# A hand-ordered opening, weight units loaded a head ahead, and where the parting of the turned weights stands

## The chip, the cores and the metric

The kernel runs on one core of one Trainium2 chip. The metric is device time in microseconds (us) of one execution. TensorE (PE) multiplies, VectorE (DVE) and ScalarE (ACT) work element by element, GpSimd (POOL) does so too[...], and SyncE (SP) issues nearly all DMA transfers. Each engine works through its own queue of instructions in order; semaphores make one wait for another.

## What is computed

One transformer layer with adaptive layer norm, all in f32, for 4 batches of 512 tokens and 256 channels. From a 4 x 256 conditioning vector `c` come six modulation vectors; two shift, two scale, two gate:

```python
mod = (_silu(L0_c) @ L0_wmod).reshape(4, 6, 1, -1)
sa, ca, ga, sb, cb, gb = (mod[:, i] for i in range(6))
ga = (2 * (ga >= 0) - 1) * jnp.maximum(jnp.abs(ga), 0.25)   # gb likewise
h = _layernorm(x) * (1 + ca) + sa
x = x + ga * attention(h)        # 16 heads of 128, causal
h = _layernorm(x) * (1 + cb) + sb
x = x + gb * ffn(h)              # top 2 of 8 experts, a shared one, a dense core
```

Attention projects h to q, k and v per head, takes a causal softmax of the scores and mixes v with it, and an output matrix W_O sums over the heads. The mixture of experts follows; the change doesn't touch its arithmetic.

## The kernel before

f32 accuracy is kept by splitting: a tensor is cast to a shorter format (`hi`), what the cast lost is subtracted out (`lo`, the helper `rest`, line 148), and three products replace one (`mm3`, lines 138 to 142: lo*hi, hi*lo, hi*hi). Weights arrive as units of 128 x 512 in one of two `stage` buffers and are split into one of ten `wu` buffers by `load_unit` (line 185): the cast by POOL (by ACT for the first three), the rest by POOL. A unit `wqk` holds a head's q and k weights; `wv` and `wo` hold two heads each.

The opening loads x of batch 0 in two pieces, `cT`, and the modulation weights (`wm`, six pieces of 256 KB). `sc` is the SiLU of `cT`: an exponential on ACT, three small steps on DVE. `modulation(0)` (line 301) multiplies it by the first pieces into `pt_mod`, whence `modT`, the shift and scale columns. `normed` (line 348) takes statistics on DVE (`bn_stats`, `bn_aggr`), 1/sqrt on POOL (`rstd`), and normalises on DVE (`xn`); `modulated` (line 378) transposes xn on TensorE into PSUM (`ptn`), applies modT there, and splits the result into `hTh` and `hTl`.

Then 64 heads follow in groups of four heads, batch after batch (line 981: heads 0 to 3 of batch 0, of batch 1, and so on). In the loop over n (line 1028) TensorE's order is written by hand:

- `weights` (line 471): four blocks of scores, 128 to 512 columns wide, in two PSUM banks taken in turn. For each: the row minimum of the negated scores on DVE (`nmax`, line 488, which frees the bank), the exponential with its row sum on ACT, its inverse on DVE, and the scaling on POOL (line 503). The generator yields after each block, so that other work stands between them.
- between the blocks: whatever `later[n]` holds, then q and then k of the next head (`project`, line 448).
- after the fourth block: `values` for the current or the next pair of heads; `finish` (line 1001, the output products of the head mixed one head before); and `mixed` (line 540), the products of v with the weights of the head three before.
- `turned` (line 506): the weights are transposed in blocks of 32 on DVE (`T`), stored to DRAM by four transfers (`moved`) and loaded again as `aT`, fully transposed. `part_one(-2)` splits the aT of two heads before (`parted`, line 531: a cast of 128 x 1152 by ACT to `aTh`, a rest by POOL).

Work beside the heads: the next batch's normalisation in heads 0 to 3 of the first group; the gates in head 1 (`make_gates`, line 319, on 4 partitions x 512); the gates' rows read back from DRAM (`gate_rows`) in heads 2 to 5; `modulation(1)` in head 6; five units loaded in heads 0 to 2; from head 18 on, feed-forward weights are split and put back to DRAM (`PART_AT`, line 102).

Only PE's order is fixed (line 151); on DVE and ACT it is fixed for the opening alone, and elsewhere a scheduler places each instruction on its engine by its own estimate of times, within `issue_after`, which keeps an instruction behind a given one.

Of the kernel before, what the change touches and what calls it, by code (L numbers as in the profile page):

```python
# [11 lines left out]
F32 = mybir.dt.float32  # L12
# [11 lines left out]
HG = 4  # L24
# [73 lines left out]
EARLY = 2  # L98


TO_PART = tuple(u for u, (_, in_parts) in UNITS.items() if in_parts)
PART_AT = (18, 20, 22, 24, 26, 28, 34, 36, 38, 40, 42)
# [11 lines left out]
def adaln_attention_moe_kernel(  # L114
# [51 lines left out]

    load_x(0, 2)
    cT = const.tile([P, DC, B], F32, tag="cT", name="cT")
    nc.sync.dma_start(cT, c_t.rearrange("(c p) b -> p c b", p=P))
# [15 lines left out]
    def load_unit(src, nm: str, early: bool = False):  # L185

        st = work.tile([P, 512], F32, tag="stage", name=f"st_{nm}")
        nc.sync.dma_start(st, src)
        u = const.tile([P, 2, 512], F32R, tag="wu", name=nm, bufs=10)
        hi, lo = u[:, 0], u[:, 1]  # L190
        if early:
            nc.scalar.copy(hi, st)
        else:
            nc.gpsimd.tensor_scalar(hi, st, 1.0, 1.0, ALU.mult, ALU.mult)
        rest(nc.gpsimd, lo, st, hi)
        return hi, lo
# [62 lines left out]
    sc_e = small.tile([P, DC, B], F32, bufs=1, tag="silu_e", name="sc_e")  # L259
    exp_c = nc.scalar.activation(sc_e, cT, AF.Exp, scale=-1.0)  # L260
    nc.vector.tensor_scalar(sc_e, sc_e, 1.0, None, ALU.add)
    nc.vector.reciprocal(sc_e, sc_e)
    sc = small.tile([P, DC, B], F32, bufs=1, tag="silu", name="sc")
    nc.vector.tensor_mul(sc, cT, sc_e)

    ct = const.tile([P, C_END], F32, tag="cols", name="cols")
    nc.gpsimd.dma_start(ct, cols)
    b1 = ct[:, C_B1:C_B2]
    with tc.issue_after(exp_c.ins):
        nc.scalar.activation(gb1, b1[:, :NCH], AF.Gelu)  # L270
    load_wm(0)
    wqk_u[0] = load_unit(wqk[0], "wqk0", True)
    wv_u[0] = load_unit(wv[0], "wv0", True)
    load_wm(1)
    load_wm(2)
    wqk_u[1] = load_unit(wqk[1], "wqk1", True)
    for b in range(1, B):
        load_x(b)
# [3 lines left out]
    nc.vector.memset(router_w, 0.0)  # L282
    nc.sync.dma_start(router_w[:, :, :E], router.rearrange("p (c n) -> p c n", n=E))
# [8 lines left out]
    nc.vector.memset(mask[:, : NT - 1, :], 0.0)  # L292
    make_causal_mask(nc, mask[:, NT - 1, :], mask_val=MASKED)
    maskf = mask.rearrange("p t k -> p (t k)")
    def mod_w(c: int, f: int, n: int) -> bass.AP:
# [5 lines left out]
    def modulation(which: int):  # L301
        pt = psum.tile([P, 4, B], F32, tag="pj", name=f"pt_mod_{which}", bufs=3)
        for i in range(4):
            for c in range(DC):
                nc.tensor.matmul(
                    pt[:, i, :],
                    lhsT=mod_w(c, 3 * D * which + i * P, P),
# [3 lines left out]
                )  # L311
        m = modT[:, 4 * which : 4 * which + 4, :]
        nc.vector.tensor_copy(m[:, :2, :], pt[:, :2, :])
        nc.vector.tensor_scalar(m[:, 2:, :], pt[:, 2:, :], 1.0, None, ALU.add)


    gates_d = dram.tile([B, 2, D], F32, tag="gates", name="gates_d")

    def make_gates():
        pm = psum.tile([B, 2, D], F32, tag="pj", name="pm", bufs=3)  # L320
        for i in range(2):
            for c in range(DC):
                nc.tensor.matmul(
                    pm[:, i, :],
                    lhsT=sc[:, c, :],
                    rhs=mod_w(c, (3 * i + 2) * D, D),
                    start=(c == 0),
                    stop=(c == DC - 1),
                )
        g = work.tile([B, 2, D], F32, tag="kh", name="g_raw")  # L330
        nc.scalar.copy(g, pm)
        sgn = work.tile([B, 2, D], F32, tag="kl", name="g_sgn")
        nc.vector.tensor_scalar(sgn, g, 0.0, 2.0, ALU.is_ge, ALU.mult)
# [866 lines left out]
```

## Time and profile before

| | |
|---|---|
| median of 3 runs | 810.0 us (808.84 to 810.09) |
| the profiled execution | 809.29 us, of which 807.5 us is the span of its instructions |
| TensorE busy | 775.5 us, 96% |
| DVE, ACT, POOL busy | 594.7, 490.9, 521.7 us |
| granted TensorE clock, mean | 0.986 |
| row minimum of the scores on DVE (line 488) | 256 x 478 ns |
| scaling of the weights on POOL (line 503) | 256 x 543 ns |
| cast of aT on ACT, its rest on POOL | 64 x 1159 ns, 64 x 2687 ns |
| moved to DRAM, and back as aT | 2.8 and 3.9 us from issue to landing |

The profile is of one execution. A row gives start and duration, the engine (PEld is TensorE's loading of the stationary operand), the source line, `out<-in` by the program's names, shapes, and in brackets how long the engine had been idle and what ended it. Matmuls are pipelined: two rows overlap, and the distance of their starts is what one costs. An f32 product that isn't split into three appears as two records.

### The profile page before, as it was taken

How to read it: one execution, taken by the hardware profiler on the slowest of the kernel's cores; microseconds unless marked ns; L12 is line 12 of the kernel's file. 1: busy time of each engine (PE TensorE's matmuls, PEld its weight loads, DVE VectorE, ACT ScalarE, POOL GpSimd, SP SyncE). 2: the span in 40 equal slices, each digit the busy share in tenths (PEclk: the TensorE clock that was granted, in tenths of full speed). 3: DMA queues.
4: the chain of work that ended last, by engine and by line, in shares of the span. 5: the costliest groups of instructions: out<-in, count | busy, mean ns of one | idle time of the engine just before them, and what ended most of it. 6: DMA issues, size and time to landing. Idle time of an engine off the chain costs nothing. (4 is left out here: it accounts for less than half of the span.)

```text
span 807.5 us, 14122 instructions
## 1 busy us (share of the span) xinstructions
PE 775.5 (96%) x4487; PEld 671.9 (83%) x4487; DVE 594.7 (74%) x1734; ACT 490.9 (61%) x1184; POOL 521.7 (65%) x523
## 2 busy tenths in 40 slices
PE   6889999999999999999999999999997999989997
PEld 5669998999999999999999999998896866767775
DVE  5968788777777667676777677778898486785665
ACT  3556667666666655666666656666656333656663
POOL 4745566896767579786758886566546155655675
PEclk9999999999999999999999999999998899999999
DMA  7465354665666667675556765545575332312221
GB/s 236 112 190 152 111 156 128 184 180 160 199 192 182 182 204 220 174 213 177 177 175 186 191 178 151 162 137 160 147 227 156 106 124 86 105 53 77 55 86 58
DMA packets 73218, 124.12 MB, mean 154 GB/s; under 512 B 8996, under 2 KB 51252, under 8 KB 73144
## 3 DMA queue, kind: packets, MB, share of 16 engines
q1 hardware_dynamic: 73112, 123.21, 52.3%
q8 instruction: 36, 0.59, 0.3%
q14 instruction: 38, 0.31, 0.1%
q0 software_dynamic: 32, 0.02, 0.0%
HBM read 73.05 MB, written 50.14 MB: 153 GB/s over the span
## 5 line engine op out<-in xcount | busy, mean ns | idle before, releaser
L148 POOL TENSOR_TENSOR aT<-aT,aTh 128x1152 fp32r<-128x1152 f32 x64 | 172.0, 2687 | 115.5 <-ACT aTh L535 115.4
L503 POOL TENSOR_SCALAR e<-e,inv 128x128 f32<-128x128 f32 (+3 forms) x256 | 135.7, 543 | 69.3 <-DVE inv L502 67.2
L498 ACT ACTIVATE e<-e,nmax 128x128 f32<-128x128 f32 (+3 forms) x256 | 143.9, 564 | 45.4 <-DVE nmax L488 44.5
L535 ACT CAST aTh<-aT 128x1152 fp32r<-128x1152 f32 x64 | 74.2, 1159 | 134.8 <-DMA aT<-moved 81.3
L488 DVE CUSTOM_DVE_ANT_0 e<-ps,mask 128x128 f32<-128x128 f32 (+3 forms) x256 | 120.1, 478 | 23.8 <-PE ps L482 14.6
L518 DVE STREAM_TRANSPOSE T<-e 128x384 f32<-128x384 f32 (+2 forms) x256 | 100.3, 445 | 7.8 <-POOL e L503 7.8
L148 DVE TENSOR_TENSOR zl<-pz,zh 128x512 fp32r<-128x512 f32 x64 | 44.0, 688 | 52.8 <-ACT zh L553 52.7
L140 PE MATMUL ps<-kh,ql 128*128 128x256 f32 (+2 forms) x192 | 71.2, 371 | 6.3 <-DVE nmax L488 6.2
L140 PE MATMUL po<-wo,zl 128*128 128x256 f32 x256 | 73.1, 285 | 0.6 <-DVE zl L148 0.6
L141 PE MATMUL po<-wo,zh 128*128 128x256 f32 x256 | 72.0, 281 | 0.0
L142 PE MATMUL po<-wo,zh 128*128 128x256 f32 x256 | 72.0, 281 | 0.0
L140 PE MATMUL pv<-wv,hTl 128*128 128x256 f32 x256 | 71.8, 281 | 0.0
L141 PE MATMUL pv<-wv,hTh 128*128 128x256 f32 x256 | 71.6, 280 | 0.0
L142 PE MATMUL pv<-wv,hTh 128*128 128x256 f32 x256 | 71.5, 279 | 0.0
L863 POOL TENSOR_TENSOR oacc<-oacc,part 128x512 f32<-128x512 f32 x28 | 40.9, 1462 | 43.5 <-DVE part L859 36.8
L502 DVE RECIPROCAL inv<-tot 128x1 f32<-128x1 f32 x256 | 40.2, 158 | 37.2 <-ACT e L498 29.6
L141 PE MATMUL ps<-kl,qh 128*128 128x256 f32 (+2 forms) x192 | 65.5, 341 | 0.2
L140 PE MATMUL pz<-aTh,vl 128*128 128x512 f32 (+2 forms) x192 | 65.5, 341 | 0.0
L141 PE MATMUL pz<-aT,vh 128*128 128x512 f32 (+2 forms) x192 | 65.4, 341 | 0.0
L142 PE MATMUL pz<-aTh,vh 128*128 128x512 f32 (+2 forms) x192 | 65.4, 340 | 0.0
L142 PE MATMUL ps<-kh,qh 128*128 128x256 f32 (+2 forms) x192 | 65.0, 339 | 0.0
L592 POOL TENSOR_TENSOR x<-x,tmp 128x512 f32<-128x512 f32 x32 | 41.4, 1298 | 19.7 <-DVE tmp L590 19.5
(216 smaller groups left out, 2327.9 us busy)
## 6 DMA issues: line engine op xcount, KB each, us to landing
moved<-T SPq DMA_DIRECT2D x256, 160.0 KB, 2.8
aT<-moved SPq DMA_DIRECT2D x64, 640.0 KB, 3.9
spread<-gates_e SPq DMA_DIRECT2D x32, 256.0 KB, 3.3
st_wqk<-in_wqk SPq DMA_DIRECT2D x16, 256.0 KB, 3.8
wf_first<-wfp_first SPq DMA_DIRECT2D x5, 512.0 KB, 5.0
st_wv<-in_wv SPq DMA_DIRECT2D x8, 256.0 KB, 3.5
st_wo<-in_wo SPq DMA_DIRECT2D x8, 256.0 KB, 3.6
wmod<-in_wmod SPq DMA_DIRECT2D x6, 256.0 KB, 5.2
```

Source lines behind the costliest of these rows:

```text
L140: nc.tensor.matmul(o, lhsT=wl, rhs=mh, start=start, stop=False)
L141: nc.tensor.matmul(o, lhsT=wh, rhs=ml, start=False, stop=False)
L142: nc.tensor.matmul(o, lhsT=wh, rhs=mh, start=False, stop=stop)
L148: return eng.tensor_tensor(lo, full, f32(hi), ALU.subtract)
L488: least = nc.vector.tensor_tensor_reduce(out=et, in0=ps[:, :n], in1=maskf[:, S - n :], scale=-SCALE, scalar=BIG, op0=ALU.add, op1=ALU.min, ...
L498: exp = nc.scalar.activation(et, et, AF.Exp, bias=nm[:, t : t + 1], scale=-1.0, accum_out=tot[:, t : t + 1])
L502: nc.vector.reciprocal(inv[:, one], tot[:, one])
L503: by_sum = nc.gpsimd.tensor_scalar(et, et, inv[:, one], 1.0, ALU.mult, ALU.mult)
L518: nc.vector.transpose(to[:, first : first + n], blocks[:, at : at + (n - 1) * step + 1 : step])
L535: nc.scalar.copy(hi, full)
L592: nc.gpsimd.tensor_tensor(xu, xu, tmp, ALU.add)
L863: recent["added"] = nc.gpsimd.tensor_tensor(oacc, oacc, to, ALU.add).ins
```

## The change

- **Opening.** Two small loads (`cols`, `cT`) go from POOL's and SP's queues to ACT's. TensorE starts with 14 products of zeros (`keep_warm`), and three more stand between the transposes and the first projections. The whole order of DVE and ACT up to q and k of head 0 is written out in `start()`: Gelu before the exponential; statistics and 1/sqrt in two halves; three normalisations on DVE and the fourth on ACT; the rest of the first unit by DVE; hTh straight from PSUM by ACT, with a separate full copy in PSUM for hTl; q and k accumulated side by side, first with hTh, last with hTl.
- **Loads.** Batch 1's x and the second unit come before the later modulation weights; x of batches 2 and 3 after the third unit. The five early units (`FIRST_UNITS`) and later all others are loaded one after another as a stage buffer comes free, and cast by ACT, at places behind named instructions.
- **Gates.** `make_gates` and `modulation(1)` become `second_modulation` in head 1, all by columns: 16 small products, and the gates' arithmetic on 128 x 16. `store_gates` in head 3 transposes them and writes them to DRAM; gates' rows are read in heads 4 to 7, and the router's weights are split in head 8.
- **Turned weights.** The splitting of aT is placed behind the last exponential and scaling of the running head; the block transposes of the third head of a batch behind the last rest of the normalisation (`recent["turned"]`).
- `PART_AT` moves by one head.

```diff
+WARM = 14
+FIRST_UNITS = (
+    ("wqk", 2, 0, 0),
+    ("wqk", 3, 0, 1),
+    ("wv", 1, 1, 0),
+    ("wo", 0, 3, 0),
+    ("wo", 1, 5, 0),
+)
-PART_AT = (18, 20, 22, 24, 26, 28, 34, 36, 38, 40, 42)
+PART_AT = (17, 19, 21, 23, 25, 27, 35, 37, 39, 41, 43)
...
+    ct = const.tile([P, C_END], F32, tag="cols", name="cols")
+    nc.scalar.dma_start(ct, cols)
+    b1 = ct[:, C_B1:C_B2]
+    cT = const.tile([P, DC, B], F32, tag="cT", name="cT")
+    nc.scalar.dma_start(cT, c_t.rearrange("(c p) b -> p c b", p=P))
     load_x(0, 2)
-    cT = const.tile([P, DC, B], F32, tag="cT", name="cT")
-    nc.sync.dma_start(cT, c_t.rearrange("(c p) b -> p c b", p=P))
...
+    def stage_unit(src, nm: str):
         st = work.tile([P, 512], F32, tag="stage", name=f"st_{nm}")
-        nc.sync.dma_start(st, src)
+        recent_dma[0] = nc.sync.dma_start(st, src).ins
+        return st
+    def part_unit(st, nm: str, early: bool, by=nc.gpsimd):
...
-        rest(nc.gpsimd, lo, st, hi)
+        if by is not None:
+            rest(by, lo, st, hi)
...
-    nc.gpsimd.dma_start(ct, cols)
-    b1 = ct[:, C_B1:C_B2]
-    with tc.issue_after(exp_c.ins):
-        nc.scalar.activation(gb1, b1[:, :NCH], AF.Gelu)
     load_wm(0)
-    wqk_u[0] = load_unit(wqk[0], "wqk0", True)
-    wv_u[0] = load_unit(wv[0], "wv0", True)
-    load_wm(1)
-    load_wm(2)
-    wqk_u[1] = load_unit(wqk[1], "wqk1", True)
-    for b in range(1, B):
-        load_x(b)
+    st_qk = stage_unit(wqk[0], "wqk0")
+    st_v = stage_unit(wv[0], "wv0")
+    load_x(1)
+    st_qk1 = stage_unit(wqk[1], "wqk1")
+    with tc.issue_after(recent_dma[0]):
+        load_wm(1)
+        load_wm(2)
...
+    def part_first(n: int, place: int):
+        while first_staged and first_staged[0][:2] == (n, place):
+            _, _, units, i, nm, st = first_staged.pop(0)
+            units[i] = part_unit(st, nm, True)
+            stage_first()
...
+    with tc.issue_after(recent_dma[0]):
+        for b in range(2, B):
+            load_x(b)
...
+    zeros = mask[:, 0, :]
+    with tc.manual_schedule(engines=fixed):
+        nc.vector.memset(mask[:, : NT - 1, :], 0.0)
+        nc.vector.memset(router_w, 0.0)
...
+    def keep_warm(n: int, tag: str):
+        pw = psum.tile([P, P], F32, tag=tag, name=f"pw_{tag}", bufs=1)
+        for _ in range(n):
+            nc.tensor.matmul(pw, lhsT=zeros, rhs=zeros, start=True, stop=True)
+    keep_warm(WARM, "av")
...
-    def modulation(which: int):
-        pt = psum.tile([P, 4, B], F32, tag="pj", name=f"pt_mod_{which}", bufs=3)
+    def by_column(pt, f: int, at: int):
...
+    def second_modulation():
+        pt = psum.tile([P, 8, B], F32, tag="pj", name="pt_mod_1", bufs=3)
+        by_column(pt, 3 * D, 0)
+        by_column(pt, 2 * D, 4)
+        set_modulation(1, pt)
...
+        nc.vector.tensor_scalar(sgn3, raw, 0.0, 2.0, ALU.is_ge, ALU.mult)
+        nc.vector.tensor_scalar(mag3, raw, -1.0, 0.25, ALU.mult, ALU.max)
+        nc.vector.tensor_tensor(mag3, mag3, raw, ALU.max)
+        nc.vector.scalar_tensor_tensor(g, sgn, 1.0, mag, op0=ALU.subtract, op1=ALU.mult)
...
+    def store_gates():
+        pg = psum.tile([GATES, P], F32, tag="pj", name="pg", bufs=3)
+        nc.tensor.transpose(pg, gates_at[0], ident)
+        rows_g = work.tile([GATES, P], F32, tag="tmp", name="g_rows")
+        nc.vector.tensor_copy(rows_g, pg)
+        nc.sync.dma_start(gates_d.rearrange("b i (c p) -> (b i c) p", p=P), rows_g)
...
-                recent["norm"] = rest(nc.vector, lo[:, d, :], whole[d], hi[:, d, :]).ins
+            nc.scalar.copy(hi[:, c, :], ptr)
+            recent["norm"] = rest(nc.vector, lo[:, c, :], ptr, hi[:, c, :]).ins
+            recent["turned"] = recent["norm"]
...
+        nc.scalar.activation(gb1, b1[:, :NCH], AF.Gelu)
+        nc.scalar.activation(sc_e, cT, AF.Exp, scale=-1.0)
+        for two in (slice(0, 2), slice(2, NT)):
+            for t in range(two.start, two.stop):
+                nc.vector.bn_stats(st[:, t, :], x0[:, t, :])
+            for t in range(two.start, two.stop):
+                nc.vector.bn_aggr(mv[:, t, :], st[:, t, :])
+            nc.gpsimd.tensor_scalar(rstd[:, two], mv[:, two, 1], LN_EPS, 1.0, ALU.add, ALU.mult)
+            nc.gpsimd.tensor_tensor(rstd[:, two], rstd[:, two], minus_half[:, two], ALU.pow)
+        nc.vector.tensor_scalar(sc_e, sc_e, 1.0, None, ALU.add)
+        nc.vector.reciprocal(sc_e, sc_e)
+        nc.vector.tensor_mul(sc, cT, sc_e)
+        pt = psum.tile([P, 4, B], F32, tag="po1", name="pt_mod_0", bufs=1)
+        by_column(pt, 0, 0)
+        wqk_u[0] = part_unit(st_qk, "wqk0", True, None)
...
+        norm(0)
+        norm(1)
+        shift = small.tile([P, 1], F32, tag="shift", name="shift_0_0", bufs=1)
+        nc.vector.scalar_tensor_tensor(
+            shift, mv[:, 3, 0:1], -1.0, rstd[:, 3:], op0=ALU.mult, op1=ALU.mult
+        )
+        last = norm(2)
+        nc.scalar.activation(xn[:, 3, :], x0[:, 3, :], AF.Identity, bias=shift, scale=rstd[:, 3:])
+        rest(nc.vector, wqk_u[0][1], st_qk, wqk_u[0][0])
+        set_modulation(0, pt)
+        with tc.issue_after(last.ins):
+            wv_u[0] = part_unit(st_v, "wv0", False)
+        hh, hl = hT[0] = tuple(
+            const.tile([P, DC, S], F32R, tag=f"hT{k}0", name=f"hT{k}_0_0") for k in "hl"
+        )
+        ptr = [psum.tile([P, S], F32, tag="pj", name=f"ptn_0_0_{c}", bufs=3) for c in range(DC)]
+        for t in range(NT):
+            for c in range(DC):
+                nc.tensor.transpose(ptr[c][:, ts(t, P)], xn[:, t, ts(c, P)], ident)
+        keep_warm(3, "av")
+        for c in range(DC):
+            scale, shift = modT[:, 2 + c, 0:1], modT[:, c, 0:1]
+            nc.scalar.activation(hh[:, c, :], ptr[c], AF.Identity, bias=shift, scale=scale)
+            full = psum.tile([P, S], F32, tag="sc", name=f"full_0_0_{c}")
+            nc.vector.tensor_scalar(full, ptr[c], scale, shift, ALU.mult, ALU.add)
+            recent["norm"] = rest(nc.vector, hl[:, c, :], full, hh[:, c, :]).ins
+        wqk_u[1] = part_unit(st_qk1, "wqk1", True)
+        pps = [
+            psum.tile([P, S], F32, tag=tag, name=f"p{nm}_0_0", bufs=bufs)
+            for nm, tag, bufs in (("q", "pj", 3), ("k", "po0", 1))
+        wh, wl = wqk_u[0]
+        for c in range(DC):
+            for w, pp in enumerate(pps):
+                at = slice((DC * w + c) * DH, (DC * w + c + 1) * DH)
+                nc.tensor.matmul(pp, lhsT=wl[:, at], rhs=hh[:, c, :], start=c == 0, stop=False)
+                nc.tensor.matmul(pp, lhsT=wh[:, at], rhs=hh[:, c, :], start=False, stop=False)
+        for c in range(DC):
+            for w, pp in enumerate(pps):
+                at = slice((DC * w + c) * DH, (DC * w + c + 1) * DH)
+                nc.tensor.matmul(
+                    pp, lhsT=wh[:, at], rhs=hl[:, c, :], start=False, stop=c == DC - 1
+                )
+        return [projected(0, 0, w, pp) for w, pp in enumerate(pps)]
+    with tc.manual_schedule(engines=fixed):
+        q, k = start()
+    values(0, 0, 0)
...
-    later[1] = [(make_gates,)]
+    later[1] = [(second_modulation,)]
+    later[3] = [(store_gates,)]
     for b in range(B):
-        later[2 + b] = [(gate_attention, b)]
-    later[2 + B] = [(modulation, 1)]
+        later[4 + b] = [(gate_attention, b)]
+    later[4 + B] = [(router_parts,)]
...
+        b, h = order[n]
+        out = []
+        if b == B - 1 and h + HG < H:
+            out.append(("wqk", h + HG))
+            if h % 2 == 0:
+                out.append(("wv", (h + HG) // 2))
+        if b == 0 and h >= HG and h % 2 == 0:
+            out.append(("wo", h // 2))
+        return out
...
-        if b == 0 and h < HG:
-            if h + 2 < HG:
-                wqk_u[h + 2] = load_unit(wqk[h + 2], f"wqk{h + 2}")
-            if h == 0:
-                wv_u[1] = load_unit(wv[1], "wv1")
-            if h in (1, 2):
-                wo_u[h - 1] = load_unit(wo[h - 1], f"wo{h - 1}")
-        for f, *args in later.pop(n, ()):
-            f(*args)
+        with ExitStack() as behind:
+            for i in (least, exp, by_sum) if n <= 2 * HG else ():
+                behind.enter_context(tc.issue_after(i))
+            part_first(n, 0)
+            for f, *args in later.pop(n, ()):
+                f(*args)
...
         if len(waiting) > 1:
-            part_one(-2)
+            with tc.issue_after(by_sum), tc.issue_after(exp):
+                part_one(-2)
...
+            if n < HG * (B - 1) and h == 2:
+                after.enter_context(tc.issue_after(recent["turned"]))
             waiting.append((b, h, turned(b, h, e)))
...
+            for units, i, nm, st in staged_units:
+                units[i] = part_unit(st, nm, True)
+        staged_units.clear()
+        for nm, i in units_of(n + 1):
+            units, src = {"wqk": (wqk_u, wqk), "wv": (wv_u, wv), "wo": (wo_u, wo)}[nm]
+            staged_units.append((units, i, f"{nm}{i}", stage_unit(src[i], f"{nm}{i}")))
+        with tc.issue_after(by_sum), tc.issue_after(exp):
+            part_first(n, 1)
...
```

## The prediction

> **What bounds the kernel now.** I read the page first (busy shares and slices), then busy time by stretch, then TensorE's waits in the first 60 us, then the rows in order of time. From the page:
>
> ```profile
> PE 775.5 (96%) x4487; PEld 671.9 (83%) x4487; DVE 594.7 (74%) x1734; ACT 490.9 (61%) x1184; POOL 521.7 (65%) x523
> ...
> PE   6889999999999999999999999999997999989997
> ...
> PEclk9999999999999999999999999999998899999999
> ```
>
> TensorE is the bound from the fifth slice on. The first slices, 20 us each, are not full; only there can an edit of the opening gain. Busy time by stretch (PE, weight loads, DVE, ACT, POOL, granted clock, DMA share, GB/s):
>
> ```profile
> 20.00:30.00 10.00, 10.00 (x53) 7.55 (x53) 8.05 (x33) 7.48 (x21) 8.18 (x12) 1.00 0.41 107
> 30.00:40.00 10.00, 7.18 (x36) 6.03 (x35) 10.00 (x27) 4.41 (x12) 6.21 (x9) 0.87 0.41 111
> 40.00:50.00 10.00, 8.36 (x45) 6.98 (x44) 6.64 (x22) 6.35 (x17) 4.70 (x6) 0.96 0.70 190
> 50.00:60.00 10.00, 8.05 (x47) 6.71 (x45) 6.94 (x24) 5.47 (x16) 4.81 (x6) 1.00 0.70 200
> 60.00:70.00 10.00, 9.89 (x54) 8.94 (x55) 8.55 (x32) 6.28 (x16) 6.07 (x7) 0.83 0.47 133
> 140.00:150.00 10.00, 10.00 (x64) 9.02 (x63) 7.18 (x25) 6.54 (x19) 9.29 (x10) 1.00 0.66 180
> ```
>
> From 30 to 60 us TensorE idles 6.4 us; at 30 to 40 DVE is full; twice the clock sags. TensorE's waits in the first 60 us:
>
> ```profile
> PE pt_mod L305 <- DVE sc L264: 6.9, 1, 6.9
> PE ps L140 <- DVE nmax L488: 2.7, 2, 1.5
> PE ps L482 <- DVE nmax L488: 1.5, 1, 1.5
> PE pq L140 <- ACT hTh L401: 0.8, 1, 0.8
> ```
>
> After the start, every wait is for a row maximum on DVE. TensorE's rows in order of time, the first product of heads 0, 2, 5, then of two late heads:
>
> ```profile
> 6.95 3.57 PE L305 MATMUL pt_mod<-sc,wmod 128*128 128x4 f32 x16 [6.95 <-DVE sc L264]
> ...
> 19.53 0.27 PE L482 MATMUL ps<-kf,qf 128*128 128x128 f32 x1
> 35.53 0.35 PE L482 MATMUL ps<-kf,qf 128*128 128x128 f32 x1 [1.50 <-DVE nmax L488]
> 68.99 0.28 PE L482 MATMUL ps<-kf,qf 128*128 128x128 f32 x1
> ...
> 79.19 1.85 PE L305 MATMUL pt_mod<-sc,wmod 128*128 128x4 f32 x16
> ...
> 164.91 0.28 PE L482 MATMUL ps<-kf,qf 128*128 128x128 f32 x1
> 174.11 0.28 PE L482 MATMUL ps<-kf,qf 128*128 128x128 f32 x1
> ```
>
> A full head takes 174.11-164.91 = 9.2 us. Undelayed products start 0.232 us apart at 512 columns, 0.175 at 384, 0.117 at 256 and 0.109 per record at 128. So a head's q and k cost 12x0.232 = 2.78, values 12x0.117 = 1.40, scores 3x(0.117+0.175+0.232)+2x0.109 = 1.79, mixing the same 1.79, output 12x0.117 = 1.40: 9.17, as measured. Head 0 has the first three, 5.98; head 1 also the gates, 7.71; head 2 eight transposes, 6.85; head 3 the mixing, 7.77; head 4 all, 9.17. Together 37.5, but they take 68.99-19.53 = 49.5. So 12 us are lost there, 3.4 of them half-speed, and 19.5 pass before.
>
> **The Trainium skill.** "TensorE: Matmul & The Clock Gate", Part 1: the clock is halved until a free-running window of 3413 ns was busy, and again after an idle one. The trace agrees: the first projections start 0.43 apart until 16.9 us and 0.23 after; the stretches at 0.87 and 0.96 lack 2x(1.3+0.4) = 3.4 us of full clock, that at 0.83 another 3.4. "ScalarE: Activation LUTs", What ACT_TABLE_LOAD costs: 1283 ns a switch; the trace has 1.28 at 0.73, 6.26 and 20.33. "GPSIMD Engine Reference", 1. Specifications: POOL shares SBUF interfaces with DVE. Four normalisations take 3.33 us at 8.05, where POOL parts weights, and 1.76 at 67.19. "DMA: Bandwidth & Descriptors", Issuing engines are not separate DMA queues: moving two loads to ACT saves issue time alone; SP spends 0.46 on cT here.
>
> **The change, part by part. (1) The opening.** Before: sc at 6.9; modulation products cold, 3.57; normalisation waits for rstd till 8.05 and ends 11.38; transposes end 12.77; hTh 13.39; q and k end at 18.11, mostly cold; values 1.42; 19.53.
> After, in the printed order: x still lands near 3.6. Statistics in halves: 3.6+1.5+0.5 = 5.6; DVE no longer waits for the exponential (1.05) between them. POOL's two halves of rstd, 0.2+1.05 each, end at 7.1. cT leaves ACT's queue near 1.9, took 3.8 before, and a second table load follows the Gelu: sc near 6.7, no gain. Zeros: fourteen f32 products are 28 records, from 1.5, once DVE has cleared the mask (0.92 to 1.30 before); at 0.218 cold (3.5 for 16 at 6.95) they hold TensorE till 7.6, 0.9 past sc. But then the modulation's 16 records cost 16x0.107 = 1.7 (as at 79.19) instead of 3.57: 9.3. Normalisations: three on DVE at 0.42 from 6.7, the fourth on ACT behind the cast of wqk0 (its load lands near 7.5): 8.9, hidden behind the modulation's products by 0.4; later than that, every us counts. Transposes 8x0.109: 10.2. hTh now straight from PSUM by ACT, 0.75, while three more zero products (0.65) fill the gap; eight products need only hTh; ACT 0.75, DVE 0.83+0.69 for each half, full behind hTh: the last hTl at 10.2+3.7, two products on: q and k end 14.6. Values: 16.0. Gain 3.5.
> What is queued behind waits there: wqk1's cast stands before q's evacuation on ACT; its load needs wqk0's stage buffer (free near 9.1), so lands near 13; cover 1 us, beyond that all is late. SP holds wmod 1 and 2 behind this load; their first reader is head 1.
> **(2) Heads 0 to 4.** The gates on DVE (0.82, 1.50, 0.67 and 0.69 at 4x512) become four of 128x16 at some 0.16: DVE loses 3.0 of its full stretch 28.8 to 40. Second modulation and gates become 32 records in head 1, 3.4, for 1.73 there plus 1.71 at 79.19: TensorE moves 1.7 forward to where it would wait. One transpose (0.1) in head 3. aT's cast no longer stands before k's evacuation (ACT waited 2.02 for its DMA at 44.66, k's rest stood 2.84 behind it, TensorE 1.49), nor POOL's 2.7 us rest before the scalings (T at 58.30 stood 0.87; TensorE 1.91). Weights are cast on ACT (0.62), which leaves POOL 1.3 for 1.9 us. The exp table is loaded once fewer (1.28 at 20.33).
> Walking the new orders with these durations: the second score product of head 0 waits 0.6 (q and k now end together, so kl is late); heads 0 to 3 then run at TensorE's pace, since the orders put the next head's two first maxima ahead of the block transposes, and the row sums, scalings and rests that DVE, ACT and POOL owe each head end 0.1 to 0.6 before their readers. From head 4 the transposes stand ahead of the maxima. Counted from head 0's first product, head 4 starts at 30.8; TensorE is ready for its third score at 32.8, which needs the bank that the first maximum frees; head 3's last scaling ends 31.7, transposes 33.2, maximum 33.4: 0.6. Head 5 starts at 40.4, would be ready at 42.4; four normalisations (1.7) and transposes (1.5) put the maximum at 43.2: 0.8. Work 5.98+9.40+6.85+7.87+9.17 = 39.3, waits 2.0: 41.3 against 49.5. Gain 8.2. wv1's rest ends 0.9 before its use; lateness there stalls head 1.
> **(3) Head 6** loses its modulation: 1.7.
> **(4) Later heads.** Casts and rests of aT move to the head's end, weight units are staged a head ahead and cast by ACT; from head 11 on TensorE waits for none of these, so they cost nothing while TensorE's 9.2 covers them; rival C prices the loss of that cover. Five router steps on DVE (0.17 each from 14.88) go to head 8; DVE is 97% busy between 100 and 110 us, so they cost between 0 and 0.8, which the 2.0 below includes. PART_AT shifts by one head, covered likewise; the loads that it issues are the same ones. On SP a stage load that waits for its buffer now stands ahead of an aT load, and gates_d with two gate loads ahead of head 2's four moved stores: some 2 us late each (2.5 to land, as 256 KB loads take 3.3 to 3.9), against a head of slack.
> Sum 3.5+8.2+1.7 = 13.4. Not seen by this walk: hops between engines, the router's steps, and idle that costs a half-speed window (1.7; even chance). For all I take off 2.0: 11.4. The profiled execution, 809.3 (span 807.5 and 1.8 around it), becomes 797.9; it stood 0.7 under the median of 810.0, so **798.5**.
> Unknowns from both sides: the zeros' warming, from all of it (gain 3.5) to none (loss 1.0, below); hop waits 0 to 4; table order -0.5 to +1.3; I take middle values.
>
> **Rivals.** A: zeros don't warm, or TensorE cools during the small products: zeros till 7.6, modulation 3.5, transposes 1.75, hTh 0.75, twelve products 5.1, values 1.4 to 2.8: 20.5, so the opening is at -1.0 for +3.5: 798.5+4.5 = 803. For: the modulation's records from 6.95 to 10.4 did not warm the clock. Against: they move four columns, the zeros 128. B: DVE stays the bound in heads 0 to 5 (it has 38 of 41 us to work: 40.2 before, less 3.0, plus 0.9); each transposed block then delays the next maximum, and (2) gains only the 3.0 of the gates: 798.5+5.2 = 803.7. C (slower): aT's rest comes too late for the mixing. The cast would start at a head's 6.3 us, the rest end 1.0 into the next; mixing begins 7.4 into it. It decides if the rest is 6.4 us later than that; each 0.3 us beyond costs 61 heads 18: 817. The move through DRAM landed 8.8 after its transposes, in time; hence improbable. D: the end of the kernel loses or gains a half-speed window: 1.7 either way.
>
> **How the numbers follow.** Forecast (796 to 801) 0.55; better, 793 to 796, 0.11; A 0.13; B 0.13; C 0.04; some other loss 0.02, nothing to see 0.02. Two in ten out: 794 to 804.5. A measurement tells 0.2% (1.6 us) from no change. Faster: 0.55+0.11+0.13+0.13 = 0.92; same 0.02; slower 0.04+0.02 = 0.06.
>
> **What would show it.** Head 0's first score product near 16.0, projections 0.23 apart; head 1 near 9.5 us long; third score product of head 5 near 57 to 60; the wait for nmax under 3 us in all before 70; head 6 near 10.2. Wrong if projections run 0.43 apart, if ACT's q evacuation stands behind wqk1's load, if head 1 waits for wv1, or if late heads exceed 9.2.

## The result, and the profile after

| | before | after |
|---|---|---|
| median of the measurement | 810.05 us (808.84 to 811.35) | 800.75 us (799.81 to 802.48) |
| ratio | | 0.9887, 95% interval 0.9865 to 0.991 |
| profiled execution, span | 809.29, 807.5 us | 800.74, 798.9 us |
| first score product of head 0 | 19.53 us | 14.98 us |
| heads 0 to 4 | 49.46 us | 43.96 us |
| head 57 | 9.19 us | 11.72 us |
| from head 63 to the end | 197.00 us | 197.99 us |

The kernel is 9.3 us faster; 11.5 were forecast, and 800.75 lies in the forecast range of 794 to 804.5. The page of the kernel after, busy times and slices:

```profile
PE 776.8 (97%) x4530; PEld 678.8 (85%) x4530; DVE 592.8 (74%) x1736; ACT 512.6 (64%) x1211; POOL 503.3 (63%) x495
...
PE   8999999999999999999999999998997989989997
...
PEclk9899999999999999999999999999998999999999
```

The first slice went from 6 to 8, the second and third from 8 to 9: TensorE is now full from the second slice on. But the second slice has a clock digit of 8. Busy time by stretch of the kernel after (PE, weight loads, DVE, ACT, POOL, granted clock, DMA share, GB/s):

```profile
20.00:30.00 10.00, 10.00 (x60) 9.42 (x59) 7.14 (x26) 4.32 (x13) 5.95 (x9) 0.73 0.41 109
30.00:40.00 10.00, 9.38 (x52) 7.92 (x51) 7.99 (x25) 6.18 (x17) 2.12 (x4) 0.93 0.40 121
40.00:50.00 10.00, 10.00 (x65) 9.12 (x64) 8.14 (x30) 9.45 (x25) 7.88 (x9) 1.00 0.46 130
50.00:60.00 10.00, 10.00 (x66) 9.13 (x65) 10.00 (x36) 5.88 (x16) 5.57 (x7) 1.00 0.87 262
60.00:70.00 10.00, 10.00 (x65) 9.05 (x64) 8.20 (x30) 7.94 (x22) 8.71 (x7) 1.00 0.61 176
140.00:150.00 10.00, 10.00 (x67) 9.22 (x66) 7.11 (x22) 7.38 (x19) 6.02 (x6) 1.00 0.70 200
```

Between 30 and 60 us TensorE idles 0.6 us, where it idled 6.4. The loss that is left is of another kind: between 20 and 40 us TensorE is busy, but 10x(0.27+0.07) = 3.4 us of clock are missing. From TensorE's waits of the kernel after, in the whole execution (us in total, times, longest; most of the rows left out lie in the feed-forward part):

```profile
PE ps L150 <- DVE nmax L540: 2.6, 2, 2.2
...
PE pw_av L332 <- DVE router L323: 1.3, 1, 1.3
...
PE ptn L440 <- DVE ql L158: 0.6, 1, 0.6
```

No wait for nmax is left before 60 us; two are left later, and one of them, 2.2 us, stood nowhere in the kernel before. TensorE's rows in order of time, kernel after: the zeros, both modulations, the first score product of heads 0, 1, 2 and 5, and then head 57:

```profile
1.30 4.73 PE L332 MATMUL pw_av<-mask 128*128 128x128 f32 x28 [1.30 <-DVE router L323]
6.32 1.95 PE L349 MATMUL pt_mod<-sc,wmod 128*128 128x4 f32 x16 [0.29 <-DVE sc L1044]
14.98 0.38 PE L534 MATMUL ps<-kf,qf 128*128 128x128 f32 x2
21.37 0.38 PE L534 MATMUL ps<-kf,qf 128*128 128x128 f32 x2
21.94 4.38 PE L349 MATMUL pt_mod<-sc,wmod 128*128 128x4 f32 x32
34.11 0.38 PE L534 MATMUL ps<-kf,qf 128*128 128x128 f32 x2
58.94 0.39 PE L534 MATMUL ps<-kf,qf 128*128 128x128 f32 x2
...
539.61 0.39 PE L534 MATMUL ps<-kf,qf 128*128 128x128 f32 x2
543.98 0.44 PE L150 MATMUL ps<-kh,ql 128*128 128x384 f32 x1 [2.24 <-DVE nmax L540]
551.33 0.39 PE L534 MATMUL ps<-kf,qf 128*128 128x128 f32 x2
```

Head 1 takes 34.11-21.37 = 12.7 us; its work is 9.4. Head 57 takes 11.7 instead of 9.2. From such rows, the whole difference of the two profiled spans, in us gained: opening 4.55; heads 0 to 4, 5.50; head 6, 1.77; head 10, 0.47; head 57, -2.53; the other heads from 5 to 62, -0.21 in sum; from head 63 to the end, -0.99. Together 8.56.

What did head 57 wait for? DVE's rows in order of time, kernel after:

```profile
538.24 4.03 DVE L413 TENSOR_SCALAR xn<-x,mv,rstd 128x256 f32<-128x256 f32 x4 [0.38 <-POOL rstd L410]
542.19 1.54 DVE L570 STREAM_TRANSPOSE T<-e 128x384 f32<-128x384 f32 x4
543.66 0.24 DVE L540 CUSTOM_DVE_ANT_0 e<-ps,mask 128x128 f32<-128x128 f32 x1
```

POOL's, at the same time:

```profile
538.30 0.83 POOL L555 TENSOR_SCALAR e<-e,inv 128x512 f32<-128x512 f32 x1
539.10 2.70 POOL L158 TENSOR_TENSOR aT<-aT,aTh 128x1152 fp32r<-128x1152 f32 x1
```

The four normalisations of batch 0's second norm take 4.03 us (1.94 at 57.19, for another batch) just while POOL subtracts in aT, in the place that the change gave it; the block transposes and the first row maximum stand behind them on DVE. Singly the four take 0.41, 0.71, 2.75 and 0.40 us: the third starts at 539.20, 0.10 us after POOL's subtraction, and ends 0.15 us after it.

So there are four questions: whether the zeros did it in the opening; what cost head 1 its clock; what cost head 57 its 2.5 us; and which part of the change freed heads 2 to 5.

### The profile page after: what moved, and what is told of

It reads as the page before. It is cut to its first block, busy times and chain, and to the rows that moved or that the text cites. A ratio compares the mean times of both kernels' runs of the same rounds, so it can differ in the third digit from the quotient of the medians.

```text
span 798.9 us, 14221 instructions
## 1 busy us (share of the span) xinstructions
PE 776.8 (97%) x4530; PEld 678.8 (85%) x4530; DVE 592.8 (74%) x1736; ACT 512.6 (64%) x1211; POOL 503.3 (63%) x495
## 4 chain that ended last, share of the span: by engine, by line
PE 88%; DVE 8%; DMA 1%; POOL 1%; issue 1%; ACT 1%; DVEq 0%; POOLq 0%; ACTq 0%
PE ps L150 4%; PE ps L151 4%; PE ps L152 4%; PE pz L150 4%; PE pz L152 4%; PE pz L151 4%; PE acc L887 4%; PE pv L150 4%; PE pv L151 4%; PE po L152 4%; PE po L150 4%; PE pv L152 4%; PE pk L150 4%; PE pk L152 4%; PE po L151 4%; PE pk L151 4%
## 5 line engine op out<-in xcount | busy, mean ns | idle before, releaser
L540 DVE CUSTOM_DVE_ANT_0 e<-ps,mask 128x128 f32<-128x128 f32 (+3 forms) x256 | 123.0, 486 | 56.3 <-PE ps L152 40.5
L605 ACT CAST zh<-pz 128x512 fp32r<-128x512 f32 x64 | 37.6, 587 | 78.9 <-PE pz L601 78.7
L158 DVE TENSOR_TENSOR al<-hid,ah 128x512 fp32r<-128x512 f32 x36 | 36.2, 1015 | 23.9 <-ACT ah L868 23.9
```

The lines of the kernel that those rows point to most:

```text
L158: return eng.tensor_tensor(lo, full, f32(hi), ALU.subtract)
L540: least = nc.vector.tensor_tensor_reduce(out=et, in0=ps[:, :n], in1=maskf[:, S - n :], scale=-SCALE, scalar=BIG, op0=ALU.add, op1=ALU.min, ...
L605: recent["z"] = nc.scalar.copy(zh.rearrange(by_block, a=NB, r=R), pz).ins
```

## The experiments

All but the last are edits of the kernel after, or that kernel itself. The ratio is to the kernel before, with its 95% interval.

### The zeros

```diff
-    keep_warm(WARM, "av")
...
-        keep_warm(3, "av")
```

> The changed kernel without its 14 and 3 products of zeros (their result is read by nothing). Theory 1, the zeros bring the clock up: without them the 16 modulation records from 6.3 us run at half speed (3.6 us instead of 1.95), the transposes (1.75 instead of 0.9) and at least the first projections 0.43 apart; first score product of head 0 near 18.5 to 19.5 instead of 14.98, time 804.5 to 805.5. Rival, the zeros do nothing for the clock or the opening's gain comes from the new order alone: first score product near 15.0 to 15.5, time 800 to 801.5. A later stretch at half speed may shift by one window (1.7 us) either way.

Measured: 802.35 us, ratio 0.9906 (0.9891 to 0.9922). TensorE's rows in the opening, without zeros:

```profile
6.30 3.60 PE L348 MATMUL pt_mod<-sc,wmod 128*128 128x4 f32 x16 [6.30 <-DVE sc L1043]
12.37 0.79 PE L1090 MATMUL pq<-hTh,wqk 128*128 128x512 f32 x1 [0.66 <-ACT hTh L1076]
12.96 0.63 PE L1091 MATMUL pq<-hTh,wqk 128*128 128x512 f32 x1
13.38 0.63 PE L1090 MATMUL pk<-hTh,wqk 128*128 128x512 f32 x1
...
18.53 0.38 PE L533 MATMUL ps<-kf,qf 128*128 128x128 f32 x2
```

The modulation takes 3.60 us instead of 1.95, the projections start 0.43 apart instead of 0.23, and the first score product comes at 18.53: 3.55 later than in the profile of the kernel after, as theory 1 has it. The rival is out. The total rose by only 1.6 and missed the expected 804.5 to 805.5. In the profiled execution head 1 lost one half-speed window (11.14 us), not two, which takes 1.6 off the 3.55; and 14.98 is the earliest first score product of eleven profiles with zeros, whose mean is 15.6. Against that mean the zeros are worth 2.9 us. Everything else in the opening is worth 1.0 against the first profile of the kernel before (19.53), 2.0 against its repeat (20.50).

### What cools the clock in head 1

First, the two groups of small products taken apart:

```diff
-        by_column(pt, 3 * D, 0)
         by_column(pt, 2 * D, 4)
-        set_modulation(1, pt)
...
+    later[2] = [(shift_and_scale,)]      # by_column(pt, 3 * D, 0); set_modulation(1, pt)
```

> The changed kernel with the 32 four-column records of head 1 parted: the 16 of the gates stay in head 1, the 16 of the second modulation go to head 2. Theory 1, a stretch of 3.4 us of four-column products lets the clock fall although TensorE never stops: with 1.7 us at a time no window is lost, heads 1 and 2 together take 17.0 to 17.5 us instead of 20.5, time 797.0 to 797.8. Rival, the half-speed stretch of 24.6 to 31.5 us comes from something else (an earlier wait, the block of head 0): heads 1 and 2 together still take 20 or more, time 800.3 to 801.3. In between (18.5 to 19, 799) if one of the two windows is still lost.

Measured: 804.28 us, ratio 0.992 (0.9892 to 0.9948): slower, which neither theory had. Up to head 3 theory 1 holds: heads 1 and 2 take 8.97+8.78 = 17.75 us and the clock is 1.00 from 20 to 40 us. But the scheduler moved some instructions of DVE and ACT around, and head 5 takes 13.09. DVE's row there, in order of time:

```profile
55.68 4.29 DVE L417 TENSOR_SCALAR xn<-x,mv,rstd 128x256 f32<-128x256 f32 x4
```

And POOL's rows of the same run:

```profile
55.55 1.28 POOL L559 TENSOR_SCALAR e<-e,inv 128x384 f32<-128x384 f32 x2
56.81 2.69 POOL L158 TENSOR_TENSOR aT<-aT,aTh 128x1152 fp32r<-128x1152 f32 x1
```

It is head 57's picture a second time, at another place: TensorE waited 2.05 us for nmax and a half-speed window followed. In the kernel after, the same four normalisations ended at 59.1 us and POOL's rest began at 60.07.

Next, the cost by itself, in head 30, far from any stall. Both kernels have the same orders on DVE, ACT, POOL and SP:

```diff
+    def repeated():
+        pr = psum.tile([P, B], F32, tag="pj", name="repeated", bufs=3)     # or [P, P]
+        for _ in range(16):
+            nc.tensor.matmul(pr, lhsT=ident, rhs=sc[:, 0, :], start=True, stop=True)  # or rhs=ident
+    later[30] = [(repeated,)]
```

> The changed kernel with 16 useless f32 products of four columns (32 records, read by nothing) added in the middle of head 30, far from any stall; DVE, ACT and POOL have the same order as in the run with 128 columns. Theory 1, such products do not keep the clock up: 32 records at 0.107 us add 3.4 us, and one or two half-speed windows of 3.4 us begin in head 30 or 31 and add 1.7 to 3.4: heads 30 and 31 together take 23.5 to 25.3 us (18.4 without). Rival, the column count does not matter: heads 30 and 31 together 21.9, full clock.

> The changed kernel with 16 useless f32 products of 128 columns (32 records, read by nothing) added in the middle of head 30. Both theories: 32 records at 0.109 us add 3.5, full clock, heads 30 and 31 together 21.9 us, time 804.2. If a half-speed window begins here too, theory 1 of the four columns falls.

Measured: 806.88 us with four columns, ratio 0.9957 (0.9941 to 0.9974); 804.43 with 128, ratio 0.9937 (0.9921 to 0.9953). TensorE's rows in order of time, four columns:

```profile
292.34 0.39 PE L534 MATMUL ps<-kf,qf 128*128 128x128 f32 x2
292.92 4.34 PE L1155 MATMUL repeated<-sc,ident 128*128 128x4 f32 x32
308.30 0.39 PE L534 MATMUL ps<-kf,qf 128*128 128x128 f32 x2
```

Its busy time by stretch, columns as above:

```profile
296.00:302.00 6.00, 6.00 (x18) 5.20 (x19) 1.29 (x4) 1.02 (x3) 0.81 (x3) 0.50 0.70 195
```

The same rows with 128 columns:

```profile
291.42 0.39 PE L534 MATMUL ps<-kf,qf 128*128 128x128 f32 x2
292.00 3.73 PE L1155 MATMUL repeated<-ident 128*128 128x128 f32 x32
304.21 0.39 PE L534 MATMUL ps<-kf,qf 128*128 128x128 f32 x2
```

And the same stretch:

```profile
296.00:302.00 6.00, 6.00 (x38) 5.40 (x37) 2.67 (x8) 3.62 (x9) 0.99 (x2) 1.00 0.65 195
```

Head 30 takes 15.96 us against 12.79, and heads 30 and 31 together 25.15 against 21.98. Behind the four-column products the clock is 0.50 although TensorE never idled; behind the wide ones it is 1.00. The records of both kinds start 0.112 us apart at full clock; what differs is the number of columns, and the values that are moved. The values hardly decide it, since products of zeros, 128 columns wide, brought the clock up in the opening. The other profiles agree: all eight with the 32 four-column records in head 1 lose one or two windows there, and the four with 16 such records or none in head 1 lose none.

The opening has an exception. In three of the eleven profiles with zeros the 16 records of the first modulation are followed by a half-speed window, and these three have the latest first score products, 16.09 to 16.77 us. In them short waits for `wmod` stretch the 16 records to 2.0 us within one window.

The Trainium skill, "TensorE: Matmul & The Clock Gate", Part 1, ties the clock to how busy TensorE has lately been; the profile counts both kinds as busy, so the share of busy time doesn't show this, only the granted clock does. The free-running window that the prediction quotes from there shows in all fourteen traces: the clock changes only at whole multiples of 3.413 us from its first rise, in the kernel after at 4.14 and then at 24.62 us, six windows on. The first rise differs by execution (6.83 us in the repeat), and with it where the 32 records fall. That would explain why they cost now one window, now two; it wasn't tested apart.

### Head 57

First the parting of aT left free in head 56 alone, as it was in the kernel before:

```diff
+            with ExitStack() as behind:
+                for i in () if n == 56 else (by_sum, exp):
+                    behind.enter_context(tc.issue_after(i))
-            with tc.issue_after(by_sum), tc.issue_after(exp):
                 part_one(-2)
```

> The changed kernel with the parting of aT left free, as before, in head 56 alone, so that POOL's 2.7 us rest no longer runs beside the four normalisations of batch 0. Theory 1, POOL's rest slows the normalisations (4.03 us) and they stand before head 57's first row maxima: the four take 1.7 to 2.3 us, head 57 takes 9.2 to 9.6 instead of 11.72, the 2.2 us wait for nmax goes, time 798.2 to 798.8. Rival, head 57 is late anyway because DVE has a whole normalisation too much in heads 56 and 57: the wait only moves, head 57 or 58 takes 11 or more, time 800.3 to 801.3.

Measured: 796.1 us, ratio 0.9832 (0.9817 to 0.9847). The normalisations take 1.37, head 57 takes 9.21 and has no wait. The total is below the range of theory 1. The profiled execution gains more than head 57's 2.5, since it also had fewer half-speed windows: one in head 1, not two, and two fewer than the kernel after from head 63 on (196.25 us there). Whether that holds for the other executions isn't shown. But the edit also moved the normalisations behind head 57's first two row maxima, so it doesn't tell the neighbour on POOL from the place in DVE's order. This does:

```diff
-        rest(nc.gpsimd, lo, full, hi)
+        if subtract:                     # n != 56
+            rest(nc.gpsimd, lo, full, hi)
```

> The changed kernel with one instruction left out: POOL's rest of aT in head 56 (that one head's mixing then uses the whole weights as their rest, a wrong sum). The orders of DVE and ACT are the same to the instruction. Theory 1, the rest slows the four normalisations beside it: they take 1.7 to 2.1 us instead of 4.03, head 57 takes 9.3 to 9.8 instead of 11.72, time 797.5 to 798.6. Rival, DVE's order (the normalisations ahead of head 57's first row maxima) is the cause: the four still take 3.5 or more, or head 57 still 11 or more, time 800 to 801.5.

Measured: 797.65 us, ratio 0.9854 (0.982 to 0.9888). DVE's rows in order of time, without that one rest:

```profile
538.75 1.68 DVE L413 TENSOR_SCALAR xn<-x,mv,rstd 128x256 f32<-128x256 f32 x4 [0.39 <-POOL rstd L410]
...
541.82 0.25 DVE L540 CUSTOM_DVE_ANT_0 e<-ps,mask 128x128 f32<-128x128 f32 x1
```

TensorE's, the first score products of heads 57 and 58:

```profile
540.11 0.39 PE L534 MATMUL ps<-kf,qf 128*128 128x128 f32 x2
549.48 0.39 PE L534 MATMUL ps<-kf,qf 128*128 128x128 f32 x2
```

With the very same order on DVE the four take 1.68 instead of 4.03, the third of them 0.40 instead of 2.75, and head 57 takes 9.37. The subtraction beside them is the cause; their place ahead of the row maxima alone doesn't cost the 2.5 us.

### Which part freed heads 2 to 5

The new place of aT's parting undone in all heads:

```diff
-            with tc.issue_after(by_sum), tc.issue_after(exp):
-                part_one(-2)
+            part_one(-2)
```

> The changed kernel with the parting of aT left free in all heads (that part of the change undone alone). Theory 1, the new place gains in heads 3 to 5 (the casts no longer before k's evacuation, 1.5 to 3.4 us) and loses 2.5 in head 57 and 0.02 us a head in pace: 799.5 to 802. Rival A, the new place is what gains most of the heads 0 to 5: heads 2 to 5 take 3.5 us or more longer, 802 to 804. Rival B, it gains nothing anywhere: heads 2 to 5 as in the changed kernel, head 57 and the pace better, 797 to 798.5.

Measured: 814.71 us, ratio 1.0062 (1.0045 to 1.0079). All three expectations were too low. Head 5 takes 16.35 us, head 10 15.12, head 28 11.68; together with heads 4 (10.42) and 6 (10.92) that is 16.6 us more than in the kernel after, and head 57's 2.5 come back. ACT's rows at the end of head 4, in order of time (head 5 starts at 58.91):

```profile
57.53 1.15 ACT L587 CAST aTh<-aT 128x1152 fp32r<-128x1152 f32 x1 [4.99 <-DMA aT<-moved]
58.59 0.26 ACT L518 COPY kf<-pk 128x128 f32<-128x128 f32 x1
```

POOL's row behind that cast, and DVE's behind POOL:

```profile
58.77 2.65 POOL L158 TENSOR_TENSOR aT<-aT,aTh 128x1152 fp32r<-128x1152 f32 x1 [5.04 <-ACT aTh L587]
...
63.30 1.94 DVE L413 TENSOR_SCALAR xn<-x,mv,rstd 128x256 f32<-128x256 f32 x4 [2.18 <-POOL rstd L410]
```

And TensorE's in head 5:

```profile
65.50 0.69 PE L150 MATMUL ps<-kh,ql 128*128 128x384 f32 x1 [3.50 <-DVE nmax L540]
```

The cast stands before k's evacuation and waits 5 us for its DMA; all of ACT waits with it. So k comes late, and so does POOL's rest of aT. Behind that rest stand a scaling and the 1/sqrt of the next normalisation; the four normalisations wait for it until 63.30, and the row maxima of head 5 stand behind them. ACT's waits for that DMA in the whole execution, with the place free:

```profile
ACT aTh L587 <- DMA aT<-moved: 74.4, 29, 5.7
```

And the page's row of the same cast in the kernel after, where the last columns are the idle time ahead of it and what ended it:

```profile
L587 ACT CAST aTh<-aT 128x1152 fp32r<-128x1152 f32 x64 | 73.1, 1142 | 3.9 <-DMA aT<-moved 3.9
```

74.4 us of waiting against 3.9 (the kernel before had 81.3). This part of the change, one `with` in the code, is worth 14 us, more than the whole; with it undone the kernel is slower than before. But that is mostly a loss which the rest of the change would bring and this part prevents: heads 5 and 28, for instance, take 9.19 in the kernel before. Heads 2 and 3 don't depend on it alone; with the place free they take 7.72 and 7.96.

The gates and the second modulation put back to their old form and place:

```diff
-    later[1] = [(second_modulation,)]
-    later[3] = [(store_gates,)]
+    later[1] = [(make_gates,)]
+    later[6].append((shift_and_scale,))
```

> The changed kernel with the gates computed as in the kernel before (on 4 partitions x 512, in head 1, without the transpose of head 3) and the second modulation in head 6 again. My step for the gates, 3.0 us of DVE's time in its full stretch: heads 1 to 4 lose 1.5 to 3.0 to waits for DVE, against which no half-speed window falls in head 1 (1.7 to 3.4 gained, since its products move 256 columns): heads 1 to 6 together 55 to 58 us (56.9 in the profile of the changed kernel), time 799.5 to 802. Rival, with the new places of casts and rests DVE's time no longer sets the pace there: heads 1 to 6 together 53.5 to 55, time 797.3 to 799.

Measured: 801.83 us, ratio 0.9894 (0.9853 to 0.9936); heads 1 to 6 57.66 us, within what was expected of the step, but not for its reason. TensorE's waits between 15 and 80 us:

```profile
PE ps L150 <- DVE nmax L541: 2.1, 1, 2.1
PE pv L151 <- POOL wv L158: 1.1, 1, 1.1
PE ps L151 <- DVE kl L158: 0.5, 1, 0.5
```

DVE is 9.86 of 10 us busy from 30 to 40 us and TensorE still waits for no row maximum in heads 1 to 4; the one wait for nmax is in head 5, where four normalisations take 4.27 us: the collision once more. Heads 1 to 4 take 34.16 us, and 33.81 in the next run, which has the new gates with the modulation likewise in head 6. So the new form of the gates is worth some 0.35 us in heads 1 to 4, not 3.0. Head 5 takes 11.59 against 9.25 there, by the collision; the orders on DVE and ACT differ between the two runs, and whether the old gates must bring it isn't shown.

What freed heads 2 and 3 therefore stays open. They took 10.50 and 9.61 us in the kernel before, and take 7.72 to 7.96 with either part undone. Both undone together, the casts of weights on ACT and the router's steps moved to head 8 weren't tried.

### A version that is faster

Head 56 left free, and the second modulation in head 6, the gates in head 1:

> As the run with head 56 left free (796.1 us), and the 16 four-column records of the second modulation moved from head 1 to head 6, where the kernel before had them; the gates' 16 stay in head 1. Theory 1, the 3.4 us stretch of four-column products costs one window at half speed in head 1 (two in the profile of the changed kernel): with 1.7 us at a time the clock stays full up to head 57, head 1 takes 7.7 to 8.0 us instead of 11.1, head 6 takes 11.8 instead of 10.1; time 794.0 to 794.8. Rival A, the window is lost for another reason and comes back elsewhere before head 6: 795.8 to 796.6. Rival B, TensorE arriving 1.7 us earlier brings the normalisations of batch 2 beside POOL's rest in head 5, as when the modulation stood in head 2: head 5 takes 12 us or more, 797.5 or more.

Measured: 795.72 us, ratio 0.9829 (0.9797 to 0.986). The clock is 1.00 from 20 to 40 us and head 1 takes 8.98 instead of 11.14, so the window is gone; head 6 takes 11.92. But heads 1 and 6 together gain 0.35 us over the run with head 56 left free, not 1.7, and the total is above theory 1's range. The earlier TensorE runs into what had been covered, as its row in head 1 shows:

```profile
29.05 0.39 PE L151 MATMUL pv<-wv,hTh 128*128 128x256 f32 x1 [0.63 <-POOL wv L158]
```

That is POOL's rest of the second wv unit. A further edit takes that unit before the fourth wqk:

```diff
-    ("wqk", 3, 0, 1),
-    ("wv", 1, 1, 0),
+    ("wv", 1, 0, 1),
+    ("wqk", 3, 1, 0),
```

> As the run with the second modulation in head 6 (795.7 us), with the second wv unit loaded and parted before the fourth wqk unit. Theory: there the values of head 1 waited 0.63 us for POOL's rest of wv1; it goes, head 1 takes 8.0 to 8.4 us instead of 8.98, and head 2's 0.63 us wait for ql stays or grows by no more than 0.3: time 794.8 to 795.4. Rival: the late unit is then wqk3, head 2 waits for it or the half-speed windows of the end move: 795.5 to 796.5.

> The changed kernel once more beside these two, so that they are compared on one chip: 800.75 us, 799.8 to 802.5 by its first measurement. Theory 1 of the four-column products expects one or two half-speed windows in head 1 again (head 1 at 11.1 or 12.7 us); without any, it falls.

Measured side by side: 797.29 us, ratio 0.9849 (0.9822 to 0.9876), and for the kernel after 800.62, ratio 0.9898 (0.9866 to 0.9929). Head 1 went to 8.11, but head 2 from 7.72 to 8.29, more than was allowed for; the opening of this profile ended at 16.55 with a half-speed window in it, and the stretch from head 63 on took 1.2 us more. So the total lies above both ranges and is no better than with the old order of units. The three versions with head 56 left free (796.1, 795.72, 797.29) can't be told from each other. The first two are below the kernel after by their intervals, and all six executions of the third (up to 797.77) are below all six of the kernel after beside it (from 799.45). The kernel after again lost a window in head 1 (11.14 us).

### The late heads

> The kernel before, once more with a profile on the chip of these runs. It tells whether the late heads' 9.21 us (9.19 in the profile shown of before) come from the change or from the chip: 9.19 again means that the change costs 0.02 us a head, some 1.2 us in all; 9.21 means that it does not.

Measured: 808.91 us, and its late heads take 9.19 again. So it comes with the change, and more exactly it is 9.213 against 9.187: 0.026 us a head, 1.0 us over 38 of the heads from 7 to 56. The other twelve, 15 to 18, 31 to 34 and 47 to 50, take 9.19 in both kernels; these are the heads that mix the weights of batch 3, from three heads before. Neither the place of aT's parting nor the gates do it: all other runs have 9.21. Where it comes from stays open. The repeated profile had its first score product at 20.50 and took 47.35 us for heads 0 to 4 with the clock full, against 49.46 in the first profile, where 3.4 us of clock were missing up to 70 us.

## Why the prediction was right, and where not

The direction and, to 2.2 us, the size came out as forecast, and none of rivals A, B and C came true as a whole: the zeros warm the clock, TensorE and not DVE bounds heads 0 to 5, no aT comes too late. That 800.75 lies even in the band of 796 to 801 is in part luck: errors of opposite sign offset each other, and executions of this kernel took 799.45 to 802.73 us. By its steps:

- **(1) The opening, 3.5.** Measured 4.55 in the profiles shown, 4.8 in the two repeats (20.50 and 15.72). Over all eleven profiles with zeros the first score product lies between 14.98 and 16.77. The term that was mis-sized is the zeros: costed cold throughout, 28x0.218 = 6.1 us, they took 4.73, because the clock rose at 4.14 us, and so did not delay the modulation, which started at 6.32 and not at 7.6. Rival A came in a small part: in three of the eleven profiles the clock fell once behind the modulation's products.
- **(2) Heads 0 to 4, 8.2.** Measured 5.5 (5.0 in the two repeats). The work was right, 39.3, and so was the sum of the waits: 1.2 us were walked through in heads 0 and 4, and by the heads' lengths 1.3 came, 0.4 in head 0 and 0.9 in head 2. The third wait of the walk, 0.8, belongs to head 5, where 0.1 came; for heads 0 to 4 alone the walk says 9.0, not 8.2. What was missed is in head 1: 3.4 us more, two half-speed windows behind the 32 four-column records that this step itself had put together. The step priced them by their row, 3.4 us, and the allowance of 2.0 held only an even chance of one window (1.7) for idling; here TensorE didn't idle. With one window, as in the repeated profile of the kernel after, heads 0 to 4 take 42.4.
- **What carries (2) was attributed wrongly in part.** The gates' 3.0 us of DVE stood first; undone, they cost 0.35 in heads 1 to 4. aT's cast and rest were to bring 1.5 and 1.9; undone, heads 3 and 4 lose 0.1 and 1.2, and heads 5, 6, 10 and 28 another 15.4. The trace of before had a sign of it: ACT waited 81.3 us in 32 places for aT. The step priced the two stalls that TensorE showed then. That more of them show once TensorE no longer comes late by itself is likely, but not shown: the orders on DVE and POOL had changed as well.
- **(3) Head 6, 1.7.** 1.77.
- **(4) Later heads, nothing.** This step failed: 2.5 us in head 57. It asked whether aT would be late for its reader, and not what POOL's 2.7 us subtraction would newly run beside. The prediction had quoted the shared interface of POOL and DVE from the Trainium skill ("GPSIMD Engine Reference", 1. Specifications), with 3.33 against 1.76 us for the same four instructions, and did not ask it again where the change moved the subtraction. The 1.0 us of the late heads were not foreseen either, though "late heads exceed 9.2" stood among the signs of being wrong.
- **Rival D.** It came in part: from head 63 on there is one half-speed window more than before, 1.0 us net. It goes by execution: 196.25 us there in one run, 200.32 in another.
- **The signs.** Head 1 was to be near 9.5 us and took 12.7. Its wait for wv1 was hidden behind the half-speed windows; once they are gone it shows, 0.63 us.
- **Two readings.** The stretches at 0.87 and 0.96 together lack 1.7 us of full clock, and the one at 0.83 another 1.7; 3.4 us is how long each ran at half speed (37.37 to 40.78 and 61.26 to 64.67). And on "ScalarE: Activation LUTs" of the Trainium skill, What ACT_TABLE_LOAD costs: the page's 1283 ns are the load alone, and it gives 2.66 us in all for a switch, with a drain. No run here shows that drain: in the kernel before a cast ends at 20.31 us, the load takes 20.33 to 21.61, and the exponential starts at 21.62.

In sum, for the two profiled executions: 4.55+5.5+1.77 = 11.8 against 13.4; the allowance of 2.0 was taken up by head 57 (-2.5), the late heads (-1.0) and the end (-1.0), less 1.3 gained in heads 10, 27 and 60 and elsewhere: 8.6.

## What to carry to other kernels

An instruction that waits for a DMA is better placed, on its in-order engine, behind all that the bottleneck needs soon. Such waits can be counted in the trace while they still cost little; here they cost 14 us once the rest of the change was in. When an instruction is moved in time, ask what it will run beside, not only who waits for it. And many small products in a row are worth spreading or taking in wider form, even where TensorE has the time for them; here the spreading alone brought little, since other waits had been covered by the lost clock.

## What the runs showed of the hardware that was not expected

- 32 records of four columns let the clock fall to half for 3.4 or 6.8 us while TensorE is busy throughout; 32 records of 128 columns do not. The records of both start 0.112 us apart at full clock. 16 records of four columns in heads 1, 2 and 6 lost no window in any run; those of the opening did in three of eleven profiles.
- Products of zeros bring the clock up: with them the projections start 0.23 us apart at 10 us (in eight of the eleven profiles), without them 0.43 apart until 16.4.
- Every change of the clock lies a whole multiple of 3.413 us from its first rise, in all fourteen traces.
- The four normalisations of 128 x 256 take 1.37 us with POOL idle (head 56 left free), 1.52 to 2.07 beside one or two of POOL's scalings, 4.02 to 4.29 when POOL's subtraction with two inputs runs beside them too. Then it is one of the four that takes 2.75, the length of the subtraction (2.70), and not all four a little more.
- The subtraction itself pays nearly nothing: it takes 2.69 and 2.70 there, 2.68 in the mean. A scaling of 128 x 512 takes 0.83 beside the normalisations and 0.70 at 548.72 without them.
